# Windowed attention and spectral feed-forward on one core: the deviation's place, five filter taps of the strip before the last image, and the taps of the last strip

## Chip, cores and metric

The kernel runs on one core of a Trainium2 chip. The metric is device time in microseconds from the first to the last instruction of the launch, with the little that lies around them. Three runs of the kernel before gave 3712.17, 3713.88 and 3715.45 us; the median is 3713.88.

## The reference, cut to what matters

The input is eight images of 384 channels and 64 x 64 points, float32. Two layers follow each other, each added to its input:

```
x = x + attention(group_norm(x))        # windows of 8x8, half of the channels shifted
x = x + feed_forward(group_norm(x))

def feed_forward(x):
    t = einsum('bchw,oc->bohw', x, w_in)
    t = irfft2(rfft2(t in 8x8 patches) * fft_filter)
    t = conv3x3(t, w_dw, one filter per channel, zero padding)
    x1, x2 = t[:, :192], t[:, 192:]
    return einsum('bchw,oc->bohw', gelu(x1) * x2, w_out)
```

The change touches only the second layer: its group norm (mean and deviation over groups of channels), the 3x3 filter with its nine taps per channel, and where these stand against each other.

## The kernel before

**Tiling.** An image is cut into NS = 8 strips of eight rows (512 points). The 384 channels are KC = 3 chunks m = 0, 1, 2 of 128 partitions. A pair (b, s) below is image b (0 to 7) and strip s (0 to 7).

**Order by hand.** Every piece of work is a function that is put into a plan with `at(place, piece, ...)`, where `place` is a number; the plan is sorted by it (L811) and the pieces are emitted in that order. An image has 16 units. The feed-forward part of image b runs beside the attention part of image b + 1, so for the last image (B - 1 = 7) it runs alone. Matrix instructions keep the program's order on TensorE (`matmul` and `transpose`, L61 to L73). For the other engines a list scheduler of the compiler decides, by its own estimate of when each instruction is ready, in what order an engine gets them; once it has decided, each engine works in order.

**The second group norm.** `second_mean` (L559) aggregates the statistics on VectorE, averages them over a group with a small matmul (`pm`) and makes a variance in a few one-column VectorE steps (`group_mean`, L241). `second_std` (L562, `group_std` L255) sends this through another matmul (`pv_`, L257), a square root on ScalarE (`sd`, L260), a reciprocal and a shift on VectorE (`sh`, L566). In the plan they stand at first + 1.25 and first + 1.90, where `first` is the unit at which an image's attention ends. For image 7 the second place comes before `back(6, 7)`, which stands at first + 1.99.

**One strip of the feed-forward part** has these steps:

- `normal_x1` (L568): three ScalarE activations to `xn`, after the deviation is known.
- `mix` (L577), four groups: matmuls to `pt`, copied to `t1` by ScalarE (L584).
- `transform` (L588), two halves: small matmuls to `pf`; VectorE multiplies by the filter into `t` (L601), four instructions.
- `back` (L605): 96 small matmuls to `pz`, one PSUM tile for each chunk, in the order 0 and 2 together, then 1. `border` (L621) copies each to a padded tile `z` on ScalarE (L629), gives the strip above its lower border row (L632), and takes the row above for the upper border (L633).
- `conv` (L658): tap by tap. The centre tap is a ScalarE activation (L667), the other eight are VectorE instructions that multiply and add (L673). `TAPS` (L638) lists the taps in the order in which they are used, centre first. Taps 6 to 8 read the row below, so they wait for the next strip.
- `gate` (L683): gelu on ScalarE (L686, L687), products on VectorE (L688 to L690).
- `finish` (L693): matmuls to `pw`, and three VectorE additions to the residual (L712, L714), then the store (L715).

**Taps on TensorE.** In the last image, some taps are matmuls with diagonal matrices: `conv_taps` (L649) sums them in PSUM, in the tile `pc`. `on_pe` (L639) says for each strip how many taps of which chunk; `conv` skips these and begins from `pc`. In strips 0 to 6 of image 7 these are five taps of chunk 1; in strip 7 all nine of chunk 1 first, and then three of chunk 2. `conv_taps(b, s)` stands at u + 2.3 (u is the strip's own unit), which is after the first of the next strip's four `mix` groups. `tap_matrices` (L642) makes the diagonal matrices with one ScalarE activation each (L646), in a strip buffer of the tag "y", of which there are three.

**PSUM.** Tiles come from two rings: four of one bank ("gemm": `pt`, `pf`, `pz`, `pw`, `pm`, `pv_`) and two of two banks ("att": `pc`, the third part of `pw`, and in attention the scores and others).

**Instruction counts.** The planner at L811 to L827 counts TensorE's instructions up to certain places (`small_tiles`, L299) and fills in empty ones (L67) so that runs of small matmuls begin at chosen positions. `conv_taps` counts there with four instructions for each tap (L814).

Of the kernel before, what the change touches and what calls it, by code (L numbers as in the profile page):

```python
# [8 lines left out]
AF = mybir.ActivationFunctionType  # L9
# [3 lines left out]
P = 128  # L13
# [5 lines left out]
NS = SW // WS  # L19
# [11 lines left out]
FETCHES = {"qk_tile": 12, "v_tile": 24, "project": 12, "scores": 128, "apply": 128, "turn": 16, "put": 16,  # L31
           "ln_sums": 64, "mix": 12, "transform": 32, "back": 192, "finish": 48, "input_mean": 4,
           "input_std": 4, "second_mean": 4, "second_std": 4, "filter_weights": 4, "out_bias": 36,
           "qk_weights": 48, "v_weights": 60}
# [4 lines left out]
def block_kernel(ctx: ExitStack, tc: tile.TileContext, out, x, consts, fsel, wqk, wv, bqk, bv,  # L39
                 wp, bp, lng, lnb, rpb1, rpb2, w_in, w_dw, w_out, filt):  # L40
    nc = tc.nc
    B = x.shape[0]
# [10 lines left out]
    def psum2(name):  # L53

        return ps.tile([P, 2, ST], F32, tag="att", bufs=2, name=name)
# [19 lines left out]
    def strip(tag, bufs, name):  # L75
        return sb.tile([P, KC, ST], F32, tag=tag, bufs=bufs, name=name)
# [12 lines left out]
    for s in range(NS):  # L89
        tag, bufs = ("x", 5) if s < 5 else (("xn", 1), ("ow", 1), ("y2", 1))[s - 5]  # L90
        t = strip(tag, bufs, f"x_first{s}")
# [4 lines left out]
    ident = cst[:, C_ID:C_ID + P]  # L96
# [48 lines left out]
    dw_sb = cp.tile([P, KC, 9], F32, name="dw_sb")  # L145
# [131 lines left out]
    def at(place, piece, *args):  # L277
        plan.append((place, len(plan), piece, args))

    xs, ys, y2s, qks, vs, os_, ots, x1s, zs = ({} for _ in range(9))  # L280
# [355 lines left out]


    TAPS = (4, 0, 1, 2, 3, 5, 6, 7, 8)  # L638
    on_pe = {s: {1: 5} for s in range(NS)}  # L639
    on_pe[NS - 1] = {1: 9, 2: 3}  # L640

    def tap_matrices():  # L642
        d = strip("y", 3, "taps").rearrange("p k (t c) -> p (k t) c", c=P)
        for m, n, to in ((1, 9, 0), (2, 3, 9)):
            for i in range(n):
                nc.scalar.activation(d[:, to + i], ident, AF.Copy, scale=dw_sb[:, m, TAPS[i]:TAPS[i] + 1])  # L646
        zs["taps"] = {1: d[:, 0:9], 2: d[:, 9:12]}

    def conv_taps(b, s):  # L649
        pc = psum2(f"pc_{b}_{s}")  # L650
        for i, (m, n) in enumerate(on_pe[s].items()):
            zs[b, s, "zz", m] = pc[:, i]
            for j in range(n):
                dy, dx = TAPS[j] // 3, TAPS[j] % 3
                matmul(pc[:, i], zs["taps"][m][:, j], zs[b, s, m][:, dy:dy + 8, dx:dx + SW],
                       start=(j == 0), stop=(j == n - 1))

    def conv(b, s, m, tap):  # L658

        z = zs[b, s, m]  # L660
        n = on_pe[s].get(m, 0) if b == B - 1 else 0
        if tap < max(n, 1):
            return
        if tap == max(n, 1):
            zz = row512("zz", 5, f"zz_{b}_{s}_{m}")
            if n == 0:
                nc.scalar.activation(zz.rearrange("p (r c) -> p r c", c=SW), z[:, 1:9, 1:SW + 1], AF.Copy,  # L667
                                     scale=dw_sb[:, m, 4:5])
                zs[b, s, "zz", m] = zz
            zs[b, s, "acc", m] = zz  # L670
        acc, old = zs[b, s, "acc", m], zs[b, s, "zz", m]
        dy, dx = TAPS[tap] // 3, TAPS[tap] % 3
        i = nc.vector.scalar_tensor_tensor(acc.rearrange("p (r c) -> p r c", c=SW),  # L673
                                           z[:, dy:dy + 8, dx:dx + SW], dw_sb[:, m, TAPS[tap]:TAPS[tap] + 1],
                                           old.rearrange("p (r c) -> p r c", c=SW), ALU.mult, ALU.add)

        if b < B - 1 and m and tap == 1:
            tc.keep_in_program_order(i)
        if b < B - 1 and (tap == 6 or m == 0 and tap == 1):
            behind(i, zs["soft"], mybir.DependencyClass.NoSync, "softmax first")  # L680
        zs[b, s, "zz", m] = acc
# [39 lines left out]
    for b in range(B):  # L721
        first = 2 * NS * b

        for s in range(NS):
            u = first - 14.84 + s if b else -10 + 0.1 * s
            at(u, load, b, s, "stats")
            at(u + (0.5 if b else 0.05), input_stats, b, s)
        if b == 0:
            at(-3.02, pack_qk)
            at(-2.9, qk_weights, 0)  # L730
            at(-0.95, v_weights)
            at(-0.94, qk_weights, 1)
            at(-0.9, position_bias, 0)
            at(-0.5, position_bias, 1)
            at(0.2, out_bias)
            at(0.2, filter_weights)
        at(first - 5.8 if b else -8, input_mean, b)
        at(first - 5.4 if b else -7.9, input_std, b)
        for s in range(NS):
            u = first + 2 * s  # L740

            v = u - 4
            at(v - 0.84, load, b, s, "norm")
            at(v + 0.15, group_normal, b, s)
            at(v + 0.45, ln_square, b, s)
            if b:
                at(v + 0.985, small_tiles, v + 1)
            at(v + 0.99, ln_sums, b, s)
            at(v + 1.35, ln_scale, b, s)

            if s:
                at(v + 1.50, shifted_half, b, s - 1, 1)
            else:
                at(u - 1.15, shifted_half, b, NS - 1, 1)
            at(u - 1.2 if s < NS - 1 else v + 1.55, shifted_half, b, s, 0)
            for br in range(2):
                w = u + br
                for t in range(3):
                    at(w - 1 + (0.14, 0.34, 0.55)[t], qk_tile, b, s, br, t)
                for g in range(2):  # L760
                    at(w - 1 + ((0.78, 0.86), (0.67, 0.88))[br][g], v_tile, b, s, br, g)
                at(w + 0.05, scores, b, s, br)
                at(w + 0.12, weights, b, s, br)
                at(w + 0.30, exponent, b, s, br)
                at(w + 0.64, turn, b, s, br)
                at(w + 1.00, apply, b, s, br)
                at(w + 1.07, normalise, b, s, br)
                at(w + 1.23, put, b, s, br)

            if 0 < s < NS - 1:  # L770
                places = [u + 3 + f for f in (0.27, 0.45, 0.70)]
            else:
                places = [first + 2 * NS + f + (0.0 if s else 0.24) for f in (0.36, 0.44, 0.52)]
            at(int(places[0]) - 0.84, load, b, s, "add")
            for m in range(KC):
                at(places[m], project, b, s, m)
            at(places[2] + 0.1, keep, b, s)
            at(int(places[2]) + 1.15, store, b, s)
        first += 2 * NS
        at(first + 1.25, second_mean, b)  # L780
        at(first + 1.90, second_std, b)
        if b == B - 1:
            at(first + 2, tap_matrices)
        for s in range(NS):
            u = first + 2 + 2 * s
            at(u - 0.84, load, b, s, "mix")
            at(u + 0.02, normal_x1, b, s)
            for i in range(4):
                at(u + (0.28, 0.45, 0.60, 0.78)[i], mix, b, s, i)
            for j in range(2):  # L790
                at(u + (0.995, 1.02)[j], transform, b, s, j)
            if b < B - 1:
                at(u + 1.985, small_tiles, u + 2)
            at(u + 1.99, back, b, s)

            for n, m in enumerate((0, 2, 1)):
                for tap in range(1, 6):
                    at(u + (2.62, 3.15, 3.5)[n] + 0.06 * tap, conv, b, s, m, tap)
                for tap in range(6, 9):
                    at(u + 4.2 + 0.25 * (n * 3 + tap - 6) / 9, conv, b, s, m, tap)  # L800
            if b == B - 1:
                at(u + 2.3, conv_taps, b, s)
            at(u + 5.16, load, b, s, "finish")
            at(u + 4.5, gate, b, s)
            at(u + 6.10, finish, b, s)
# [5 lines left out]
    order = [p[2:] for p in sorted(plan, key=lambda p: p[:2])]  # L811
    count, dense, empty = fetched["count"], [], [0] * len(order)
    for i, (piece, args) in enumerate(order):
        count += 4 * sum(on_pe[args[1]].values()) if piece is conv_taps else FETCHES.get(piece.__name__, 0)  # L814
        if piece in (qk_tile, project):
            dense.append(i)
        elif piece is scores:
            dense = []
        elif piece is small_tiles:
            n = (RUN_AT[args[0] % 2] - count - round(WAITS[0] * args[0] + WAITS[1])) % 256  # L820
            if n < 100:
                count += n
                for j in range(n):
                    empty[dense[j % len(dense)]] += 1
# [111 lines left out]
```

## Time and profile before

| what | value |
|---|---|
| median of three runs | 3713.88 us |
| the profiled execution, device time | 3717.37 us |
| its span, first to last instruction | 3715.4 us |
| mean granted TensorE clock | 0.995 |
| busy PE (matmuls) | 3609.1 us, 97% |
| busy DVE (VectorE) | 2844.0 us, 77% |
| busy ACT (ScalarE) | 2383.0 us, 64% |
| busy POOL (GpSimd) | 435.1 us, 12% |
| VectorE taps L673 in the whole run | 1490, 751 ns mean |
| `pc` matmul records (two for each tap) | 94 |
| tap matrices L646 | 12, median 410 ns |

The profile is of one execution, 3.49 us above the median of the three runs. Names in it are those of the engines (PE is TensorE, PEld its weight loads, DVE VectorE, ACT ScalarE, POOL GpSimd, SP the queue of DMA issues) and of the program's tiles. A timeline line has the start in us, the time in us, engine, line, operation, output and inputs, shapes, and how many instructions were merged; in brackets how long the engine was idle before and what ended that. Merged instructions of one kind overlap a little, so the start-to-start time is shorter than the mean duration.

Image 7's feed-forward part takes the last 220 us or so. Its eight last additions and stores come one a strip until the end at 3715.4.

### The profile page before, as it was taken

What the parts mean: (1) busy time and instruction counts of PE and PEld (TensorE: products, weight loads), DVE (VectorE), ACT (ScalarE), POOL (GpSimd) and SP (SyncE); (2) the same over time, 40 slices, a digit from 0 to 9 for tenths busy, and PEclk for the clock granted to TensorE, in tenths of its full rate; (3) what the DMA queues carried; (4) which work ended last, traced back from release to release, by engine and by line L of the source; (5) the groups of instructions that cost most, each with busy time, mean ns of one, the idle gap of its engine ahead of it and who ended that gap; (6) DMA issues with size and microseconds to landing.
All of it is one profiled execution on the core that took longest, in us unless ns stands there. A gap on an engine that the chain in (4) does not pass through costs nothing.

```text
span 3715.4 us, 92922 instructions
## 1 busy us (share of the span) xinstructions
PE 3609.1 (97%) x38528; PEld 2340.4 (63%) x38528; DVE 2844.0 (77%) x4601; ACT 2383.0 (64%) x3946; POOL 435.1 (12%) x776
## 2 busy tenths in 40 slices
PE   4999999999999999999999999999999999999898
PEld 2666666666666666666666666666666666666554
DVE  4555568777887788787887778877788777777898
ACT  1766676666676576675776667676676766676442
POOL 5111111011111011101111011111011111110000
PEclk9999999999999999999999999999999999999999
DMA  4222222233232233222332332323232322222422
GB/s 122 80 89 75 92 100 102 87 111 109 101 123 84 89 134 109 104 94 104 107 130 84 109 106 101 132 82 105 88 131 102 107 89 84 100 81 81 154 103 77
DMA packets 144507, 377.34 MB, mean 102 GB/s; under 512 B 12308, under 2 KB 12900, under 8 KB 144100
## 3 DMA queue, kind: packets, MB, share of 16 engines
q1 hardware_dynamic: 139952, 370.60, 28.4%
q8 instruction: 319, 5.23, 0.6%
q0 software_dynamic: 2048, 0.15, 0.1%
q10 hardware_dynamic: 2100, 0.63, 0.1%
q14 instruction: 88, 0.72, 0.1%
HBM read 270.54 MB, written 100.79 MB: 100 GB/s over the span
## 4 chain that ended last, share of the span: by engine, by line
PE 86%; DVE 6%; DMA 4%; ACT 2%; issue 1%; POOL 0%; SPq 0%; DVEq 0%; ACTq 0%; POOLq 0%
PE pq L62 24%; PE pr L62 13%; PE pvv L62 12%; PE pt L62 12%; PE pw L62 6%; DVE zz L673 3%; PE pS L62 3%; PE pA L62 3%; PE pT L72 3%; PE po L72 3%; PE pz L62 3%; PE pf L62 2%; PE ln L62 2%; DMA x_norm<-in_x_dram 1%; DMA rpb_raw<-in_rpb_dram 1%
## 5 line engine op out<-in xcount | busy, mean ns | idle before, releaser
L673 DVE SCALAR_TENSOR_TENSOR zz<-z,dw_sb,zz 128x512 f32<-128x512 f32 x1490 | 1081.8, 751 | 23.7 <-ACT z L632 11.2
L62 PE MATMUL pq<-y,wqk_sb 128*128 128x512 f32 x2160 | 990.2, 596 | 0.0
L62 PEld LDWEIGHTS pq<-y,wqk_sb 128*128 128x128 f32 x2160 | 402.7, 190 | 437.1 <-issue 403.9
L62 PE MATMUL pt<-wi_sb,xn 128*128 128x384 f32 x1536 | 534.6, 486 | 0.0
L62 PE MATMUL pr<-oT,wp_sb 128*128 128x512 f32 x1152 | 523.1, 592 | 0.4 <-DVE oT L537 0.4
L62 PE MATMUL pvv<-wv_sb,y 128*128 128x192 f32 x2880 | 495.8, 326 | 0.0
L62 PEld LDWEIGHTS pvv<-wv_sb,y 128*128 128x128 f32 x2880 | 471.7, 190 | 36.2 <-issue 22.0
L394 ACT ACTIVATE qab<-pq,bq_sb,cst 96x512 f32<-96x512 f32 (+1 forms) x256 | 197.8, 772 | 401.9 <-PE pq L62 385.0
L62 PEld LDWEIGHTS pt<-wi_sb,xn 128*128 128x128 f32 x1536 | 286.1, 190 | 200.9 <-issue 44.0
L394 ACT ACTIVATE kcd<-pq,vec 32x512 f32<-32x512 f32 x512 | 348.4, 680 | 9.0
L62 PEld LDWEIGHTS pr<-oT,wp_sb 128*128 128x128 f32 x1152 | 211.1, 190 | 223.8 <-issue 212.3
L376 POOL COPY y<-y 128x384 f32<-128x384 f32 x112 | 100.0, 893 | 1529.4 <-PE pvv L62 1035.9
L335 POOL TENSOR_TENSOR sq<-sq 128x512 f32<-128x512 f32 x128 | 164.3, 1283 | 638.2 <-ACT sq L333 633.3
L584 ACT COPY t<-pt 128x384 f32<-128x384 f32 x256 | 124.1, 485 | 177.7 <-PE pt L62 174.5
L667 ACT ACTIVATE zz<-z,dw_sb 128x512 f32<-128x512 f32 x183 | 134.0, 733 | 159.0 <-PE pw L62 144.5
L349 DVE TENSOR_TENSOR lr<-m 128x128 f32<-128x128 f32 x64 | 19.7, 308 | 278.3 <-ACT m L347 278.3
L394 ACT ACTIVATE qcd<-pq,bq_sb,cst 96x512 f32<-96x512 f32 (+1 forms) x256 | 197.1, 770 | 44.4 <-PE pq L62 40.9
L428 ACT COPY v<-pvv 128x384 f32<-128x384 f32 x256 | 120.7, 477 | 160.2 <-PE pvv L62 159.2
L546 DVE SCALAR_TENSOR_TENSOR x_add<-pr,vec,x_add 128x512 f32<-128x512 f32 x192 | 143.4, 747 | 94.3 <-PE pr L62 92.6
L62 PE MATMUL pw<-zz,wo_sb 128*128 128x512 f32 (+1 forms) x512 | 182.4, 499 | 0.0
L394 ACT ACTIVATE kab<-pq,vec 96x512 f32<-96x512 f32 (+1 forms) x256 | 174.2, 680 | 9.0 <-PE pq L62 7.4
L72 PEld LDWEIGHTS pT<-cst,e 128*128 128x128 f32 x1024 | 119.1, 141 | 67.2 <-issue 39.8
(140 smaller groups left out, 5297.2 us busy)
## 6 DMA issues: line engine op xcount, KB each, us to landing
x_add<-in_x_dram SPq DMA_DIRECT2D x64, 768.0 KB
x1d<-x_add SPq DMA_DIRECT2D x64, 768.0 KB
x_mix<-x1d SPq DMA_DIRECT2D x64, 768.0 KB
x_finish<-x1d SPq DMA_DIRECT2D x64, 768.0 KB
out_dram<-x_finish SPq DMA_DIRECT2D x64, 768.0 KB
x_norm<-in_x_dram SPq DMA_DIRECT2D x61, 768.0 KB
x_stats<-in_x_dram SPq DMA_DIRECT2D x56, 768.0 KB
rs<-line SPq DMA_DIRECT2D x62, 256.0 KB
```

The costliest lines, as they stand in the source:

```text
L62: tc.keep_in_program_order(nc.tensor.matmul(*args, **kw))
L72: tc.keep_in_program_order(nc.tensor.transpose(*args, **kw))
L335: nc.gpsimd.tensor_tensor(sq[:, 0, :], sq[:, 0, :], sq[:, k, :], ALU.add)
L349: nc.vector.tensor_tensor(rc, m[:, 0:P], m[:, 0:P], ALU.mult)
L376: nc.gpsimd.tensor_copy(dst[:, :, :, :, 0:4], src[:, :, :, :, 4:8])
L394: return nc.scalar.activation(dst[to:to + n], pq[of:of + n], AF.Identity, bias=bias[of:of + n], scale=scale)
L428: nc.scalar.copy(v[:, 2 * g:2 * g + 2, :, 0:HD], pvv[:, 0:384].rearrange("p (g h d) -> p g h d", g=2, h=4))
L546: nc.vector.scalar_tensor_tensor(t[:, m, :], pr, bp_sb[:, m:m + 1], t[:, m, :], ALU.add, ALU.add)
L584: nc.scalar.copy(t1, pt[:, 0:C])
L667: nc.scalar.activation(zz.rearrange("p (r c) -> p r c", c=SW), z[:, 1:9, 1:SW + 1], AF.Copy, scale=dw_sb[:, m, 4:5])
L673: i = nc.vector.scalar_tensor_tensor(acc.rearrange("p (r c) -> p r c", c=SW), z[:, dy:dy + 8, dx:dx + SW], dw_sb[:, m, TAPS[tap]:TAPS[tap] ...
```

## The change

Three edits are made together.

- For image 7, `second_std` moves from first + 1.90 to first + 1.995, which is behind `back(6, 7)` (first + 1.99) and the instruction-count place between them, and before `tap_matrices` and `normal_x1(7, 0)`.
- `on_pe` gets pairs (image, strip) as keys. Strip (6, 7), the last of image 6, which was wholly on ScalarE and VectorE, now has five taps of chunk 1 on TensorE as well. `conv_taps(6, 7)` stands between the first and the second `mix` group of (7, 0).
- In the last strip (7, 7) TensorE takes five taps of chunk 2 in place of three, and these come before chunk 1's nine. `tap_matrices` makes 14 matrices in place of 12, in two buffers of the tag "y" in place of one.

```diff
     TAPS = (4, 0, 1, 2, 3, 5, 6, 7, 8)
-    on_pe = {s: {1: 5} for s in range(NS)}
-    on_pe[NS - 1] = {1: 9, 2: 3}
+    on_pe = {(B - 1, s): {1: 5} for s in range(NS - 1)}
+    on_pe[B - 2, NS - 1] = {1: 5}
+    on_pe[B - 1, NS - 1] = {2: 5, 1: 9}
 
     def tap_matrices():
         d = strip("y", 3, "taps").rearrange("p k (t c) -> p (k t) c", c=P)
-        for m, n, to in ((1, 9, 0), (2, 3, 9)):
+        d2 = strip("y", 3, "taps2").rearrange("p k (t c) -> p (k t) c", c=P)
+        for m, n, to in ((1, 9, d), (2, 5, d2)):
             for i in range(n):
-                nc.scalar.activation(d[:, to + i], ident, AF.Copy, scale=dw_sb[:, m, TAPS[i]:TAPS[i] + 1])
-        zs["taps"] = {1: d[:, 0:9], 2: d[:, 9:12]}
+                nc.scalar.activation(to[:, i], ident, AF.Copy, scale=dw_sb[:, m, TAPS[i]:TAPS[i] + 1])
+        zs["taps"] = {1: d[:, 0:9], 2: d2}
 
     def conv_taps(b, s):
         pc = psum2(f"pc_{b}_{s}")
-        for i, (m, n) in enumerate(on_pe[s].items()):
+        for i, (m, n) in enumerate(on_pe[b, s].items()):
...
     def conv(b, s, m, tap):
 
         z = zs[b, s, m]
-        n = on_pe[s].get(m, 0) if b == B - 1 else 0
+        n = on_pe.get((b, s), {}).get(m, 0)
...
         at(first + 1.25, second_mean, b)
-        at(first + 1.90, second_std, b)
+        at(first + (1.90 if b < B - 1 else 1.995), second_std, b)
...
-            if b == B - 1:
+            if (b, s) in on_pe:
                 at(u + 2.3, conv_taps, b, s)
...
-        count += 4 * sum(on_pe[args[1]].values()) if piece is conv_taps else FETCHES.get(piece.__name__, 0)
+        count += 4 * sum(on_pe[args].values()) if piece is conv_taps else FETCHES.get(piece.__name__, 0)
```

## The prediction

> **What bounds the kernel now.** The page gives TensorE 97% of the span, but the change acts only on the last 220 us, so I read first the busy time by stretch (columns: stretch, its length, then busy us and instruction count of PE, PEld, DVE, ACT, POOL, then granted clock, DMA share, GB/s).
>
> ```profile
> 3350.00:3400.00 50.00, 50.00 (x553) 32.82 (x552) 37.34 (x58) 32.38 (x56) 3.75 (x8) 1.00 0.23 80
> ...
> 3500.00:3550.00 50.00, 40.04 (x391) 25.82 (x393) 49.26 (x81) 21.50 (x41) 0.15 (x1) 0.90 0.45 161
> 3550.00:3600.00 50.00, 48.18 (x483) 29.39 (x476) 44.51 (x71) 22.71 (x53) 0.00 (x0) 0.97 0.30 109
> ```
>
> Up to 3450 TensorE is full. In 3500 to 3550, the seam before image 7's feed-forward part, VectorE is full and TensorE lacks 10 us, and its clock drops. Then I read the timeline of TensorE at the seam.
>
> ```profile
> 3499.70 0.38 PE L62 MATMUL pm_b<-mv_b,cst 128*128 128x1 f32 x2
> 3504.28 0.56 PE L62 MATMUL pv_b<-gt_b,cst 128*128 128x1 f32 x2 [4.19 <-DVE gt_b L252]
> 3504.77 3.68 PE L62 MATMUL pz<-cst,t 64*64 64x64 f32 x96
> ...
> 3520.79 1.53 PE L62 MATMUL pf<-t,cst 64*64 64x192 f32 x32
> 3525.55 3.99 PE L62 MATMUL pz<-cst,t 64*64 64x64 f32 x94 [3.23 <-DVE t L601]
> ```
>
> The deviation's matmul pv_b holds the finished work of back(6,7) behind a VectorE chain (4.19 us). The next hole, 3.23 us, is a wait for t(7,0), which VectorE takes only after eight taps:
>
> ```profile
> 3518.70 6.33 DVE L673 SCALAR_TENSOR_TENSOR zz<-z,dw_sb,zz 128x512 f32<-128x512 f32 x8
> 3524.95 1.94 DVE L601 TENSOR_TENSOR t<-pf,feff 128x384 f32<-128x384 f32 x4
> ```
>
> So the seam is bound by VectorE. Last, all engines in the last two strips: a regular strip's hand-over, then the end.
>
> ```profile
> 3657.55 4.72 DVE L673 SCALAR_TENSOR_TENSOR zz<-z,dw_sb,zz 128x512 f32<-128x512 f32 x7 [1.57 <-ACT z L632]
> ...
> 3667.59 6.71 DVE L673 SCALAR_TENSOR_TENSOR zz<-z,dw_sb,zz 128x512 f32<-128x512 f32 x10
> ...
> 3674.88 1.94 DVE L601 TENSOR_TENSOR t<-pf,feff 128x384 f32<-128x384 f32 x4
> ...
> 3678.39 4.73 DVE L673 SCALAR_TENSOR_TENSOR zz<-z,dw_sb,zz 128x512 f32<-128x512 f32 x7 [1.57 <-ACT z L632]
> ...
> 3682.54 10.47 PE L62 MATMUL pc<-z,taps 128*128 128x512 f32 x24
> ...
> 3688.44 6.32 DVE L673 SCALAR_TENSOR_TENSOR zz<-z,dw_sb,zz 128x512 f32<-128x512 f32 x8
> ...
> 3692.94 1.52 PE L62 MATMUL pw<-g,wo_sb 64*64 64x512 f32 x16
> ...
> 3700.83 0.74 DVE L673 SCALAR_TENSOR_TENSOR zz<-z,dw_sb,zz 128x512 f32<-128x512 f32 x1
> 3701.66 0.63 ACT L687 ACTIVATE g<-zz 64x512 f32<-64x512 f32 x1 [6.24 <-DVE zz L673]
> ...
> 3703.07 3.56 PE L62 MATMUL pw<-g,wo_sb 64*64 64x512 f32 x16 [5.83 <-DVE g L688]
> ...
> 3709.64 0.69 DVE L714 TENSOR_TENSOR x_finish<-pw,x_finish 128x512 f32<-128x512 f32 x1 [0.17 <-PE pw L62]
> ```
>
> A strip takes 20.84 us (3657.55 to 3678.39). Ten taps that alternate between chunks take 0.67 us each; eight of one chunk, each on the last one's sum, 0.79. A tap on TensorE is two records of 0.433 us (24 in 10.4), so 0.87. At the end the chain is chunk 2's taps on VectorE, gelu, gate, and then a pw at less than half speed (3.56 for 1.52).
>
> **The change, part by part.** *Matrices.* Fourteen instead of twelve, 0.41 us each on ScalarE, and a second buffer. The twelve ran at 3312 to 3319, long before use, while TensorE was busy 10.00 of each 10 us. The two more should fill in likewise at no cost; uncovered they cost 0.8. The five of the second buffer can come a strip later, still 150 us early. Four more empty instructions of 13 ns follow from the kernel's own count. No DMA is added or moved, nothing passes SP or POOL.
>
> *Deviation behind back(6,7).* The four t before it end at 3501.04 and free its PSUM. A regular strip runs the rest of pz in 1.45 us, so pz ends near 3502.7. pv_b still waits for gt_b (3504.13) and starts at 3504.28 as before; behind it in TensorE's queue stand finish(6,5) and all of image 7. But pz is out of the way: pw can start at 3504.6 and, taking 4.3, end at 3509. The square root on ScalarE now stands near three z evictions. If they go first (to 3504.3) and a table load of 1.28 follows, sd is at 3505.6; before, 2.3 us from sd to the first xn and 2.3 for three gave 3511.3, so now 3510.2. If sd goes first, the evictions hold pw's PSUM to about 3506.6 and pt starts at 3511. Either way pt, before at 3512.95, gains 2 to 2.8; I take 3510.2.
>
> *Five taps of (6,7).* TensorE adds 5 x 0.87 = 4.3 us, after the first of four mix groups. z is there (evicted by 3507). pf comes at 3510.2 + 1.94 + 4.3 + 5.8 = 3522.2, 1.4 later than before; its first half is done at 3523.0. VectorE loses four taps, 4 x 0.67 = 2.7 us, and ScalarE one 0.72 us activation, which has idle time around it. What is late next is t(7,0). Bounds: it keeps its place at 3524.95, or chunk 1's four taps come before it, as they do in regular strips (ten taps, the one that reads pc, then t). By the nearest row, that strip, I take the second: 12 alternating taps from 3518.70, 12 x 0.67, put t at 3526.7. TensorE then idles from 3523.7 to 3527.2 and its clock falls: from t to pw it took 4.29 us here before (3524.95 to 3529.24). So pw(6,6) is at 3531.0, the next pf half 17.2 later as before (3529.24 to 3546.44), and t(7,1) at 3548.4 with 0.17 of hand-over. VectorE would be ready at 3545.3 (19 taps, three adds, three gate products after t), so TensorE decides. From t to the strip's first tap is 3.51, one strip more 20.84: 3572.8, where the trace has 3574.16. **Seam: 1.4 us.** The five strips after it keep their period and pass this on.
>
> *Last strip.* Chunk 2's five taps come first in pc, chunk 1's nine after. Counted in the old times, pc takes 28 x 0.433 = 12.1 to 3694.7 (1.7 more), pw(7,6) another 4.3 to 3699.0. VectorE has 8 + 4 taps in place of 8 + 6, and chunk 2 starts once five taps are done at 3686.9, so the chunks alternate: 3688.44 + 12 x 0.67 = 3696.5, three gate products of 0.7 to 3698.6. So pw(7,7) follows pw(7,6) without a hole at 3699.0 instead of 3703.07: 4.1. No hole, no clock drop: from pw's start to the last add 4.3 instead of 6.57 (3703.07 to 3709.64): 2.2. The 5.8 us from that add to the end stay. **Tail: 6.3 us.**
>
> *The clock.* In this trace the clock stood at 0.50 after holes of 4.19, 3.23 and 5.83 us, and also after one of 2.39 (3547.2 to 3549.6):
>
> ```profile
> 3548.00:3549.00 1.00, 0.00 (x0) 0.00 (x0) 1.00 (x3) 0.38 (x1) 0.00 (x0) 1.00 0.00 0
> 3549.00:3550.00 1.00, 0.41 (x26) 0.41 (x29) 1.00 (x3) 0.00 (x0) 0.00 (x0) 0.99 0.76 111
> 3550.00:3551.00 1.00, 0.72 (x28) 0.53 (x20) 1.00 (x3) 0.00 (x0) 0.00 (x0) 0.50 0.76 295
> ```
>
> The holes of 0.6 us in regular strips leave it at 1.00. The Trainium skill, "TensorE: Matmul & The Clock Gate", Part 1, says that half clock comes after an idle window of some 3.4 us. By that rule a tail that leaves TensorE idle 1.7 us stays fast; by the rows it lies between 0.6 and 2.39 and may lose the 2.2. The rule speaks against me at the seam, where 3.5 us idle is slow by either. With 2.0 idle instead (t in its old place), the rule would leave 3.45 from t to pw, the row 4.29; I keep both as ends.
>
> **The sum.** 1.4 + 6.3 = 7.7 us of the span of 3715.4, giving 3707.7. The profiled run's device time of 3717.37 has 2.0 outside the span, untouched: 3709.7. It stands 3.5 above the median 3713.88, so the forecast in those terms is 3706.2.
>
> **Rivals.** *t keeps its place* (0.25). Before, it came right after chunk 0's eight taps, which speaks for it; the regular strips speak against. t(7,1) is then at 3546.2 (VectorE 3545.9, TensorE 3545.8 to 3546.6), the seam gives 3.6, total 9.9: 3704.0.
>
> *The gate is late at the end* (0.22). VectorE might take the three residual adds of (7,6), which end near 3700, before the gate, or not read chunk 2 until all of pc is done. The old order, with two taps between and behind those adds, speaks for it; the idle engines speak against. pw(7,7) at 3700.7 saves 4.6 with a fast clock, 2.4 with a slow one: 3707.9 or 3710.1.
>
> *The added TensorE taps eat the seam* (0.09): t(7,0) at 3528 gives nothing at the seam, 3707.6.
>
> *The deviation becomes the wait* (0.04), on the other side. ScalarE works in order; if the root is queued behind the gelu pair of gate(6,6) (before to 3514.5) and reloads its table, sd is at 3515.8, pt at 3520.3, pf's half at 3533.1, t(7,1) at 3555.0, the seam 5.2 slower. With the tail at its low end (1.3, two taps) that is 3.9 slower, 3717.8. It turns against the kernel once sd is later than about 3512. Against it: pv_b's matmul is ready eight microseconds before that pair.
>
> My forecast has 0.40. What a measurement can tell from no change is about 0.2%, 7.4 us, so the forecast is only just beyond it: two thirds of its chance, nearly all of the first rival and little else make faster 0.56; slower by that much needs the last rival and more, 0.03; the rest, 0.41, lies within. The range reaches from 3703.0 (the first rival, a little better) to 3710.6 (the slow-clock tail).
>
> **What would show it.** The hole before pv_b shrinks to some 1.6 us with pz ahead of it; twelve taps with one reading pc stand between gate(6,6) and t(7,0); the strips keep 20.84; pc has 28 records in the last strip; no hole before the last pw and a clock of 1.00 to its end. I am wrong if t(7,0) stands elsewhere, if a hole of over 2 us stays before the last pw, or if ScalarE runs sd after the gelu pair.

## The result, and the profile after

| | before | after |
|---|---|---|
| median, us | 3712.44 (3707.72 to 3715.63, 17 runs) | 3705.64 (3703.85 to 3710.05, 17 runs) |
| ratio after / before, 95% interval | | 0.9984 (0.9977 to 0.999) |
| the profiled execution: device time, span, us | 3717.37, 3715.4 | 3707.98, 3705.9 |

The ratio says 5.9 us less (0.0016 x 3712), from 3.7 to 8.5; the two medians differ by 6.8. The spans of the two profiled executions differ by 9.5 us, which is more than the change did; the profiled execution of before (3717.37) is slower than all of its 17 timed runs. Image 6's last strip shows how far the two executions were apart by then: its first filter product `t` (L601) starts at 3494.25 after and at 3499.09 before. Nearly all of that was there far earlier: the same reciprocal of image 6's attention (the 100th of 128 on L503), ahead of anything in which the two programs differ, starts at 2703.28 and 2707.94. So 4.84 us of the 9.5 are taken here as belonging to the execution, not to the kernel. So I measure from that product onward, in two pieces: the **seam**, from it to the first filter tap behind the last strip's z (the row of seven taps with "<-ACT z L632"), and the **tail**, from there to the end of the span.

| us | seam | tail | both |
|---|---|---|---|
| before | 179.30 | 37.01 | 216.31 |
| after | 176.39 | 35.26 | 211.65 |
| gain | 2.91 | 1.75 | 4.66 |

To set a time of after beside one of before, add 4.84. First the busy time by stretch, in the columns of the table before.

```profile
3500.00:3550.00 50.00, 45.78 (x397) 26.71 (x390) 46.49 (x74) 23.16 (x45) 0.00 (x0) 0.97 0.42 152
3550.00:3600.00 50.00, 48.34 (x396) 28.04 (x395) 46.47 (x74) 19.87 (x44) 0.00 (x0) 1.00 0.34 120
```

At the seam TensorE now works 45.78 of 50 us where it worked 40.04, and VectorE is no longer full. Since after is 4.84 us ahead, each window lies that much further into the work than before's, so these rows show a direction, not an amount. The timeline of TensorE has the amounts.

```profile
3495.33 2.54 PE L62 MATMUL pz<-cst,t 64*64 64x64 f32 x96
3499.35 0.38 PE L62 MATMUL pv_b<-gt_b,cst 128*128 128x1 f32 x2 [1.48 <-DVE gt_b L252]
...
3504.97 2.32 PE L62 MATMUL pt<-wi_sb,xn 128*128 128x384 f32 x6 [1.01 <-ACT xn L574]
3507.12 4.46 PE L62 MATMUL pc<-z,taps 128*128 128x512 f32 x10
...
3517.32 1.53 PE L62 MATMUL pf<-t,cst 64*64 64x192 f32 x32
3521.35 3.66 PE L62 MATMUL pz<-cst,t 64*64 64x64 f32 x95 [2.51 <-DVE t L601]
```

The wait before `pv_b` is 1.48 us where it was 4.19, since the 96 matmuls of `pz` now stand ahead of it; `pv_b` itself is no earlier (3504.19 in before's times, 3504.28 then). `pt` of (7,0) is 3.14 us earlier. The five taps, ten records, use that up, and `pf` is 1.37 later. The hole before `pz` of (7,0) is 2.51 where it was 3.23. VectorE's timeline shows why it is not longer.

```profile
3513.29 0.69 DVE L691 TENSOR_TENSOR g<-g,zz 64x512 f32<-64x512 f32 x1
3513.99 0.75 DVE L675 SCALAR_TENSOR_TENSOR zz<-z,dw_sb,zz 128x512 f32<-128x512 f32 x1
3514.66 0.74 DVE L675 SCALAR_TENSOR_TENSOR zz<-z,dw_sb,pc 128x512 f32<-128x512 f32 x1
3515.32 5.51 DVE L675 SCALAR_TENSOR_TENSOR zz<-z,dw_sb,zz 128x512 f32<-128x512 f32 x8
3520.74 1.95 DVE L601 TENSOR_TENSOR t<-pf,feff 128x384 f32<-128x384 f32 x4
...
3542.03 1.95 DVE L601 TENSOR_TENSOR t<-pf,feff 128x384 f32<-128x384 f32 x4 [1.47 <-PE pf L62]
```

Ten taps, with one that reads `pc`, stand between the gate of (6,6) and `t`(7,0), which starts 0.63 us later than before (3525.58 against 3524.95). `t`(7,1) waits 1.47 us for `pf`, so at that point TensorE decides. Last, TensorE and VectorE at the end of the kernel, put together by time.

```profile
3674.79 12.18 PE L62 MATMUL pc<-z,taps 128*128 128x512 f32 x28
3680.69 6.33 DVE L675 SCALAR_TENSOR_TENSOR zz<-z,dw_sb,zz 128x512 f32<-128x512 f32 x8
3687.01 0.75 DVE L675 SCALAR_TENSOR_TENSOR zz<-z,dw_sb,pc 128x512 f32<-128x512 f32 x1
...
3692.13 1.07 PE L62 MATMUL pw<-g,wo_sb 64*64 64x512 f32 x2 [0.93 <-DVE g L690]
3694.17 1.95 PE L62 MATMUL pw<-g,wo_sb 64*64 64x512 f32 x14 [0.97 <-DVE g L691]
3696.04 4.06 PE L62 MATMUL pw<-zz,wo_sb 128*128 128x512 f32 x8
```

VectorE runs chunk 0's eight taps in a row, at 0.79 us each from start to start, and reads chunk 2 from `pc` for the first time at 3687.01. `pc`'s five taps of chunk 2 were done some 4.3 us after 3674.79; its last record ends at 3686.97. The last `pw` is held twice by the gate, and then runs slowly: the clock granted (the third number from the end) falls just there.

```profile
3694.00:3695.00 1.00, 0.83 (x8) 0.35 (x11) 0.11 (x1) 0.00 (x0) 0.00 (x0) 1.00 0.38 145
3695.00:3696.00 1.00, 1.00 (x9) 0.21 (x3) 0.00 (x0) 0.00 (x0) 0.00 (x0) 0.56 1.03 389
3696.00:3697.00 1.00, 1.00 (x4) 0.50 (x2) 0.00 (x0) 0.00 (x0) 0.00 (x0) 0.50 0.69 252
```

### The profile page after: what moved, and what is told of

It is laid out like the page before. It is cut to its first block, busy times and chain, and to the rows that moved or that the text cites. A ratio compares the mean times of both kernels' runs of the same rounds, so it can differ in the third digit from the quotient of the medians.

```text
span 3705.9 us, 92947 instructions
## 1 busy us (share of the span) xinstructions
PE 3610.6 (97%) x38542; PEld 2337.9 (63%) x38542; DVE 2839.0 (77%) x4595; ACT 2382.8 (64%) x3947; POOL 435.2 (12%) x776
## 4 chain that ended last, share of the span: by engine, by line
PE 86%; DVE 6%; DMA 4%; ACT 2%; issue 1%; POOL 0%; SPq 0%; DVEq 0%; ACTq 0%; POOLq 0%
PE pq L62 25%; PE pr L62 13%; PE pvv L62 12%; PE pt L62 12%; PE pw L62 6%; DVE zz L675 3%; PE pS L62 3%; PE pA L62 3%; PE po L72 3%; PE pT L72 3%; PE pz L62 3%; PE pf L62 2%; PE ln L62 2%; DMA x_norm<-in_x_dram 2%; DMA rpb_raw<-in_rpb_dram 1%
```

## The experiments

Every edit is shown against the kernel after, if nothing else is said. Seam and tail come from one profiled execution each, the ratio to before from timed runs. e5 and e7 have one time each, which tells nothing at this size. A seam is known no better than to about 1 us: the six kernels with the same seam (after, e1, e2, e6, e7, e9) range from 175.62 to 176.78, the two with the old one (before, e5) from 179.30 to 180.00.

| | seam | tail | both: gain on 216.31 | median, us (runs) | ratio, 95% interval |
|---|---|---|---|---|---|
| after | 176.39 | 35.26 | 4.66 | 3705.64 (17) | 0.9984 (0.9977 to 0.999) |
| e2 both seam edits | 176.78 | 36.87 | 2.66 | 3710.93 (12) | 0.999 (0.9981 to 0.9998) |
| e3 deviation alone | 177.68 | 37.62 | 1.01 | 3711.76 (12) | 0.9992 (0.9984 to 1.0001) |
| e4 five taps of (6,7) alone | 179.27 | 38.17 | -1.13 | 3713.29 (12) | 1.0 (0.9991 to 1.0008) |
| e5 last strip alone | 180.00 | 33.61 | 2.70 | 3713.45 (1) | |
| e1 after, own bank for chunk 2 | 175.66 | 30.55 | 10.10 | 3703.87 (6) | 0.9972 (0.9961 to 0.9984) |
| e6 own bank, three taps | 176.62 | 32.25 | 7.44 | 3706.01 (11) | 0.9979 (0.997 to 0.9987) |
| e7 gate before the additions | 176.78 | 33.04 | 6.49 | 3706.56 (1) | |
| e8 own bank, filter first | 176.82 | 30.58 | 8.91 | 3704.01 (12) | 0.9975 (0.9966 to 0.9983) |
| e9 own bank, four taps | 175.62 | 31.10 | 9.59 | 3702.99 (11) | 0.9975 (0.9966 to 0.9984) |
| e10 own bank, seven taps of (6,7) | 176.85 | 30.63 | 8.83 | 3703.68 (8) | 0.9976 (0.9966 to 0.9986) |

The gain read from one trace and the ratio, turned into us, agree within 2.0 us in each timed kernel (e1: 10.10 and 10.4; e2: 2.66 and 3.7; e3: 1.01 and 3.0; e4: -1.13 and 0). Much of what is left is the clock: before, e2, e3 and e4 have the same last strip, yet their tails run from 36.87 (e2) to 38.17 (e4), as the last eight records of `pw`, behind the same hole of 5.8 us, take 2.93 us in e2 and 4.25 in e4.

### The last strip: what holds chunk 2

**e1** gives chunk 2 a PSUM tile of one bank, in place of its half of the two-bank tile `pc`, which chunk 1 then has alone. The matmuls, their order and their number stay.

```diff
-            zs[b, s, "zz", m] = pc[:, i]
+            own = psum(f"pc2_{b}_{s}") if m == 2 else pc[:, 0]
+            zs[b, s, "zz", m] = own
...
-                matmul(pc[:, i], zs["taps"]...
+                matmul(own, zs["taps"]...
```

> The changed kernel, but chunk 2's five taps of the last strip get a PSUM tile of their own of one bank, in place of a half of the two-bank tile that they share with chunk 1's nine. Measured from the first filter product t(6,7) to the end of the span, which was 216.31 us before and 211.65 with the change. Theory A: in the last strip VectorE takes chunk 2's taps only after all of pc, because the shared tile ties them to chunk 1's matmuls; with its own tile the two chunks alternate at 0.67 us a tap, the gate is done before pw(7,6) ends, no hole and no clock drop follow, and the tail gains the 6.3 us of the prediction in place of 1.75: about 207.1 us, faster than the changed kernel by some 4.5 us. Theory B: VectorE's amount of work, or the later pw on TensorE, sets the tail whatever the order: within 0.7 us of 211.65.

The timeline of e1's last strip, both engines put together:

```profile
3673.70 12.18 PE L62 MATMUL pc<-z,taps 128*128 128x512 f32 x28
3679.59 0.75 DVE L676 SCALAR_TENSOR_TENSOR zz<-z,dw_sb,zz 128x512 f32<-128x512 f32 x1
3680.25 0.74 DVE L676 SCALAR_TENSOR_TENSOR zz<-z,dw_sb,pc 128x512 f32<-128x512 f32 x1
3680.91 4.72 DVE L676 SCALAR_TENSOR_TENSOR zz<-z,dw_sb,zz 128x512 f32<-128x512 f32 x7
...
3687.23 0.69 DVE L692 TENSOR_TENSOR g<-g,zz 64x512 f32<-64x512 f32 x1
3687.26 2.85 PE L62 MATMUL pw<-zz,wo_sb 128*128 128x512 f32 x8
3690.03 1.55 PE L62 MATMUL pw<-g,wo_sb 64*64 64x512 f32 x16
3690.18 0.69 DVE L693 TENSOR_TENSOR zz<-zz,pc 128x512 f32<-128x512 f32 x1 [0.70 <-ACT zz L689]
3691.52 2.85 PE L62 MATMUL pw<-zz,wo_sb 128*128 128x512 f32 x8
```

Chunk 2 is read from PSUM at 3680.25, 5.6 us before `pc`'s last record ends (3673.70 + 12.18 = 3685.88; the trace calls both tiles `pc`). The chunks alternate at 0.67 us, the gate's first two products are done while the `pw` before is still running, the third (L693) ends at 3690.87, and the last `pw` follows without a hole in 1.55 + 2.85 us. The tail is 6.46 us shorter than before, and the time from `t`(6,7) to the end is 206.21, where 207.1 was expected. So the tie was the tile: by it, the read of one half waits for matmuls into the other. The waits in VectorE's compiled program say the same. TensorE raises its counter to 20262 with chunk 2's fifth tap, and to 20271 with chunk 1's ninth. These are the two instructions that read `pc`, and the counts that they wait for, first in the kernel after, then in e1:

```
L675 TensorScalarPtr zz_7_7_2<-z1,dw_sb,pc_7_7 [waits PE 20271]
L692 TensorTensor zz_7_7_0<-zz_7_7_0,pc_7_7 [waits Activation 3748]

L676 TensorScalarPtr zz_7_7_2<-z1,dw_sb,pc2_7_7 [waits PE 20262]
L693 TensorTensor zz_7_7_0<-zz_7_7_0,pc_7_7 [waits PE 20271, Activation 3749]
```

In after, the read of chunk 2 waits for chunk 1's ninth tap, though the two halves are different banks; in e1 it waits for its own fifth. The second read of after has no wait for TensorE of its own, as the first has already waited for all of the tile. So the wait is one that is written into the program when it is built. The scheduler's order changed with it, though nothing but the tile had changed: in after it puts chunk 0's eight taps ahead of the read. VectorE therefore never stands idle there, and the tie shows in no wait of the profile: it shows as an order.

**e5** is the change of the last strip alone (the deviation back at first + 1.90, no taps of (6,7)).

```diff
-    on_pe[B - 2, NS - 1] = {1: 5}
...
-        at(first + (1.90 if b < B - 1 else 1.995), second_std, b)
+        at(first + 1.90, second_std, b)
```

> Only the last strip's taps changed (five of chunk 2 first, then nine of chunk 1), deviation and strip (6,7) as before. Two lengths: the seam from t(6,7) to the first tap after the last strip's z (179.3 us before, 176.4 with the change), and the tail from there to the end (37.0 before, 35.3 with the change; two more kernels with the old tail gave 36.9 to 38.2). Theory A, the two parts are separate: seam 179.3, tail 35.3 within 0.7, with chunk 2's taps behind all of pc and two holes of about 1 us before and in the last pw. Rival: the tail's gain needs the shifted seam, so the tail is 36.5 or more.

The tail was 33.61, 1.65 less than after's with the same last strip, and below the range of 34.6 to 36.0 that was expected. The holes are the same, what differs is the clock in the `pw` behind them:

```profile
3699.28 1.07 PE L62 MATMUL pw<-g,wo_sb 64*64 64x512 f32 x2 [0.93 <-DVE g L689]
3701.32 1.51 PE L62 MATMUL pw<-g,wo_sb 64*64 64x512 f32 x14 [0.97 <-DVE g L690]
3702.77 2.85 PE L62 MATMUL pw<-zz,wo_sb 128*128 128x512 f32 x8
```

Here the last two rows take 1.51 and 2.85 us, in after 1.95 and 4.06: 1.65 together, all of the difference. The new last strip is worth 1.75 or 3.4 us against the trace of before, by this alone.

**e6** is e1 with the old number, three taps of chunk 2 (still ahead of chunk 1's nine).

```diff
-    on_pe[B - 1, NS - 1] = {2: 5, 1: 9}
+    on_pe[B - 1, NS - 1] = {2: 3, 1: 9}
```

> The changed kernel with chunk 2's PSUM tile of its own, but only the old three taps of chunk 2 on TensorE in the last strip. With five taps and its own tile the tail was 30.6 us, with five and the shared tile 35.3. Theory A, it is the tie to chunk 1's matmuls that cost the prediction its tail, not the number of taps: VectorE has two taps more, 1.3 us, but TensorE's pc is 1.7 us shorter, so the tail stays within 30.4 to 31.6. Rival, the two taps taken from VectorE are what counts: a tail of 32 to 33.5.

The number is the rival's, 32.25 us, with three holes of 0.53 to 0.74 us before parts of the last `pw`, as here the first of them:

```profile
3692.13 1.07 PE L62 MATMUL pw<-g,wo_sb 64*64 64x512 f32 x2 [0.73 <-DVE g L691]
```

The own bank with the old number of taps (and with chunk 2's taps ahead of chunk 1's, where before has them behind) thus brings 4.76 us of tail, the taps without the own bank 1.75 to 3.4, both together 6.46. All of these are counted from before's tail, in which the clock was slow. So both count, and the own bank counts for more.

**e7** leaves the tile as it is and puts the residual additions of (7,6) behind the gate of (7,7) in the plan, a test of the other half of the rival in the prediction.

```diff
-            at(u + 6.10, finish, b, s)
+            at(u + (6.60 if (b, s) == (B - 1, NS - 2) else 6.10), finish, b, s)
```

> The changed kernel (shared tile), with finish(7,6) planned behind gate(7,7), so that one of the residual additions of strip (7,6) goes behind the last gate product on VectorE in place of before it; TensorE's order is the same. With the change the last pw has holes of 0.93 and 0.97 us and the tail is 35.3. Theory A, the second hole is that addition: it falls to 0.4, and the tail to about 34.6; if less idle time also spares the clock drop, to 33.3. Rival, TensorE's own pace or the output's store sets the end: 35.3 unchanged.

The tail is 33.04.

```profile
3692.41 0.69 DVE L690 TENSOR_TENSOR g<-g,zz 64x512 f32<-64x512 f32 x1 [0.15 <-ACT g L689]
3693.13 0.69 DVE L714 TENSOR_TENSOR x_finish<-pw,x_finish 128x512 f32<-128x512 f32 x1
3693.85 0.69 DVE L691 TENSOR_TENSOR g<-g,zz 64x512 f32<-64x512 f32 x1
```

Against e5, which ran at the same full clock, that is 0.57 us, and VectorE's rows give the same: between the gate's two products now stands one addition, not two, and the second product starts 1.44 us after the first (3692.41 to 3693.85) instead of 2.04 in after. So this one addition costs 0.6 us. Two more still stand ahead of the second product, one before the first and one between; what they cost was not run. In e1 all three stand behind the gate's first two products, with no edit to the plan: chunk 2 is done before `pw`(7,6) is, so there is nothing yet to add. What e1 gains over e7, 2.49 us, holds both the tile and those two.

**e9** asks whether e1 takes one tap too many. It is e1 with one less.

```diff
-    on_pe[B - 1, NS - 1] = {2: 5, 1: 9}
+    on_pe[B - 1, NS - 1] = {2: 4, 1: 9}
```

> As the own-bank kernel, with four taps of chunk 2 on TensorE in the last strip instead of five (13 taps in all, 26 records). With five, TensorE set the end: the gate's last product ended at 3687.92 and the last pw could begin at 3690.03, 2.1 us of slack on VectorE. Theory: one tap fewer gives TensorE 0.87 us back and costs VectorE 0.67, so the slack shrinks to 0.6 and TensorE still sets the end: tail 29.7 us (30.55 with five, 32.25 with three), no hole of over 0.3 us before the last pw. Rival: VectorE already sets the end with four, as it does with three: holes of 0.5 us before the last pw and a tail of 30.9 to 31.5.

The rival is right by its number: 31.10, with a hole of 0.99 us, not in front of the last `pw` but inside it.

```profile
3688.94 1.29 PE L62 MATMUL pw<-g,wo_sb 64*64 64x512 f32 x8
3691.22 0.66 PE L62 MATMUL pw<-g,wo_sb 64*64 64x256 f32 x8 [0.99 <-DVE zz L693]
```

The gate's two products are early enough, as I had worked out; what is late is L693, the one that reads chunk 1 from `pc`, behind chunk 0's gelu. I had measured the slack at the wrong instruction: in e1 L693 ends at 3690.87, not 3687.92. The third part of the last `pw` waits for it, as it takes its PSUM from the same ring of two tiles as `pc`: in e1's compiled program its first matmul waits for the count that L693 sets. e9's timed ratio can't be told from e1's.

### The seam: two edits, alone and together

**e2** is both seam edits with the old last strip, **e3** the deviation alone, **e4** the five taps of (6,7) alone.

```diff
e2
-    on_pe[B - 1, NS - 1] = {2: 5, 1: 9}
+    on_pe[B - 1, NS - 1] = {1: 9, 2: 3}
e3, beyond e2
-    on_pe[B - 2, NS - 1] = {1: 5}
e4, beyond e2
-        at(first + (1.90 if b < B - 1 else 1.995), second_std, b)
+        at(first + 1.90, second_std, b)
```

> The deviation's move and the five taps of (6,7), with the last strip as before (chunk 1's nine taps first, then three of chunk 2). From t(6,7) to the end. Theory A, from the changed kernel's trace: the seam alone gives 2.9 us and the last strip the other 1.75: 213.4 us, with pw of the last strip again behind a hole of 5.8 us and slow. Rival: the last strip only shows what it has because the seam shifted it against the clock's window; then the sum does not split like this and this run is off 213.4 by more than 0.7 us.

> Only the deviation moved behind back(6,7). From t(6,7) to the end, 216.31 before. Theory A, VectorE binds the seam: TensorE reaches pf(7,0) about 3 us sooner, but VectorE has the same work before t(7,1), so the time only lengthens the next hole: 215.5 to 216.3 us. Rival, TensorE's hole of 4.2 us was itself the loss: about 213.3 us.

> Only the five taps of (6,7) on TensorE, deviation and last strip as before. From t(6,7) to the end, 216.31 before. Theory A: without the deviation's move the 4.3 us of added matmuls meet a TensorE that is 3 us later, pf(7,0) comes at about 3525.1 in old times and VectorE takes t(7,0) behind twelve taps near 3528, so little is left: 215.1 to 215.8 us; the two edits of the seam are worth more together than one by one. Rival, they add up: 2.7 us of VectorE work removed shows in full, about 213.6 us.

Gains at the seam: 2.52 for both, 1.62 for the deviation, 0.03 for the taps. Both together bring 0.87 more than the sum, which is within what one execution can be off; the timed ratios (3.7 us for both, 3.0 for the deviation, 0 for the taps) do not part e2 from e3 either. e4 missed both of its ranges: 217.44 from `t`(6,7) to the end, where 215.1 to 215.8 was expected and 213.6 was the rival; 1.16 us of that arise in its tail, where the same last `pw` ran at a slower clock than in before. e3 lies 0.2 below its range (215.30, for 215.5 to 216.3). TensorE's timeline of e3 shows what the deviation alone leaves open:

```profile
3505.92 8.13 PE L62 MATMUL pt<-wi_sb,xn 128*128 128x384 f32 x24 [1.01 <-ACT xn L574]
...
3542.31 4.56 PE L62 MATMUL pz<-cst,t 64*64 64x64 f32 x94 [2.41 <-DVE t L601]
3546.56 1.12 PE L62 MATMUL pw<-g,wo_sb 64*64 64x512 f32 x2
...
3549.36 2.85 PE L62 MATMUL pw<-zz,wo_sb 128*128 128x512 f32 x8
```

Before has at the same place:

```profile
3549.59 0.84 PE L62 MATMUL pz<-cst,t 64*64 64x64 f32 x32 [2.39 <-DVE t L601]
3550.72 2.89 PE L62 MATMUL pz<-cst,t 64*64 64x64 f32 x62 [0.28 <-DVE t L601]
...
3554.89 2.85 PE L62 MATMUL pw<-zz,wo_sb 128*128 128x512 f32 x8
```

In e3, `t`(7,0) comes 3.9 us sooner, counted from `t`(6,7), 22.0 against 25.86. The four taps it overtook are still VectorE's work, and a strip later the hole before `pz` of (7,1) is 2.41 us, no shorter than before's 2.39. It ends 3.4 us sooner than before's (47.11 against 50.50 from `t`(6,7)). But from there to the last eight records of `pw` it takes 7.05 us, and 5.30 before: the clock stood at 0.50 for 6.8 us, and for 3.4 before. So half of what the deviation had won was lost to the clock in this execution. And of e4:

```profile
3500.05 0.35 PE L62 MATMUL pv_b<-gt_b,cst 128*128 128x1 f32 x2 [4.20 <-DVE gt_b L252]
...
3523.95 1.30 PE L62 MATMUL pf<-t,cst 64*64 64x192 f32 x14 [2.05 <-ACT t L584]
```

The first hole is as it was, and the 4.3 us of taps come on top of it: `pf` is late. On top of that, half of it waits 2.05 us for ScalarE's copy, which stands behind the gelu in ScalarE's order. So the taps alone bring nothing that can be seen, since `pf` is late; the later deviation gives TensorE the room for them. That they add to the deviation is not shown. Had the clock of e3 stayed down no longer than before's, its gain would be some 3.4 us (an estimate, 1.62 + 7.05 - 5.30), where both edits gave 2.52 to 3.68.

**e8** asks which engine sets the seam in after. It is e1 with chunk 1's taps of (6,7), and taps 6 to 8 of the other chunks, put behind the filter product `t`(7,0) by a dependency on order alone.

```diff
-            nc.vector.tensor_tensor(t2[:, p], pf_[p]...
+            zs["filtered"] = nc.vector.tensor_tensor(t2[:, p], pf_[p]...
...
+        if (b, s) == (B - 2, NS - 1) and tap >= (5 if m == 1 else 6):
+            behind(i, zs["filtered"], mybir.DependencyClass.NoSync, "filter first")
```

> Own PSUM tile for chunk 2 as in the first of these runs (seam 175.7 us, tail 30.6), and in strip (6,7) chunk 0's taps 6 to 8 and chunk 1's taps are ordered behind t(7,0) on VectorE, so that TensorE's hole of 2.5 us before back(7,0) and its slow clock go. Theory A, VectorE's work binds the seam: t(7,0) comes 2.5 us sooner and TensorE with it, but VectorE idles about 1.4 us for pf and has the same taps left before t(7,1): seam 175.5 to 177. Rival, TensorE's chain from t(7,0) to t(7,1) binds: seam about 173.4. The tail is 30.6 in both.

As expected if VectorE sets it: 176.82, and not the 173.4 of a seam that TensorE sets. `t`(7,0) starts 24.00 us after `t`(6,7) instead of 26.49, the hole before its `pz` is gone, and another of 3.10 us opens a strip later, with no idle time of VectorE ahead of `t`(7,1):

```profile
3519.78 0.69 PE L62 MATMUL pz<-cst,t 64*64 64x64 f32 x32 [0.48 <-DVE t L601]
...
3543.05 3.65 PE L62 MATMUL pz<-cst,t 64*64 64x64 f32 x94 [3.10 <-DVE t L601]
```

**e10** then takes work from VectorE: e1 with seven taps of (6,7).

```diff
-    on_pe[B - 2, NS - 1] = {1: 5}
+    on_pe[B - 2, NS - 1] = {1: 7}
```

> As the own-bank kernel, with seven taps of chunk 1 of strip (6,7) on TensorE instead of five. Theory: VectorE's total work sets the seam, and TensorE only waits there (2.50 us before the pz of (7,0)). Two taps fewer take 1.3 us from VectorE and put 1.7 us of TensorE work into that hole, which shrinks to 1 us or less, so that the clock stays at 1.00: from t(6,7) to the last strip's first tap behind its z 174.3 to 175.0 us (175.66 with five here, 176.39 in the kernel after). Rival: TensorE's chain through pf sets it, and two taps more push t(7,0) back: 176.5 to 177.4. The tail should stay at 30.6 in both.

It missed: 176.85, 1.2 us longer than with five. The rows of TensorE, then of VectorE:

```profile
3521.09 0.88 PE L62 MATMUL pf<-t,cst 64*64 64x192 f32 x14 [1.40 <-ACT t L584]
3522.38 0.69 PE L62 MATMUL pz<-cst,t 64*64 64x64 f32 x32 [0.42 <-DVE t L601]
```

```profile
3541.95 1.95 DVE L601 TENSOR_TENSOR t<-pf,feff 128x384 f32<-128x384 f32 x4 [2.02 <-PE pf L62]
```

The hole before `pz` is filled, as meant, but `pf` of (7,0) is pushed back and waits for ScalarE, as in e4, and at `t`(7,1) VectorE stands idle for 2.02 us. So e8 and e10 lie on either side of the balance: with the filter earlier VectorE decides, with more taps on TensorE the chain through `pf` does. They do not lie equally far off. Counted from `t`(6,7), `t`(7,1) starts at 47.03 in e1, 47.28 in e8 and 48.23 in e10. e10 has its whole 1.2 us by then; e8 has 0.25, and the other 0.9 arise behind the hole of 3.10 us, where `pz` runs at half clock.

## Why the prediction was right, and where it was wrong

The forecast of 3706.2 lies 0.56 us from the median of 3705.64, and its gain of 7.7 us within the interval of 3.7 to 8.5. Yet its two terms are not what the runs show: the seam gave about twice its 1.4 us, the last strip a quarter to a half of its 6.3. The agreement is in good part luck: two errors met, and the median of before, from which the forecast was counted, fell from 3713.88 in three runs to 3712.44 in seventeen.

**Matrices: right.** The fourteen ran from 3308.1 to 3364.1, 390 ns each in the median, long before their use.

**Deviation behind back(6,7): right, step by step.** `pv_b` was not to move, and did not (0.09 us). ScalarE took the three z evictions first, then the square root with its table load, which is the order of the two that I had taken. `pt` was put at 3510.2 and came at 3509.81 in before's times. The rival in which the root is queued behind the gelu pair did not occur.

**Five taps of (6,7): the mechanism right, a term too large.** `pf` was put at 3522.2 and came at 3522.16. I let twelve taps follow the gate of (6,6); there were ten, since of chunk 0's eight one ran ahead of the gate and one behind `t`. So `t`(7,0) came at 3525.58, not 3526.7, the hole was 2.51, not 3.5, and `t`(7,1) came at 3546.87, not 3548.4. The seam's gain was 2.91 (2.52 in e2, with a slower clock; 3.64 in e1, at full clock). The rival "t keeps its place" was near by its number (3.6), but not by its order: `t` came 0.63 later, behind chunk 1's taps.

**Last strip: the step that failed** is "chunk 2 starts once five taps are done at 3686.9, so the chunks alternate". Chunk 2 started when all fourteen were done. Of the gate rival I had written "or not read chunk 2 until all of `pc` is done", and gave it 0.22 together with the residual additions. e1 shows that this clause is what kept the tail from its 6.3 us, and e7 that one of the three additions is worth 0.6 us. The rival had put the tail's gain at 4.6 with a fast clock and 2.4 with a slow one; it measured 3.4 (e5) and 1.75 (after). What I should have asked is not when the data are there but what the program waits for: a tile of two banks is one thing to wait for, and the text of the kernel shows that both chunks share it. With the own bank the same arithmetic came true: 6.46 for 6.3.

**The clock: a range too simple.** I put the limit for a slow clock between holes of 0.6 and 2.39 us. Two holes of 0.93 and 0.97, 1.1 us apart, were enough in after and not in e5; the last section shows that the length of a hole is not all that counts.

**Time.** e1, with the own bank, has the lowest ratio: 0.9972 of before, where the change has 0.9984. Their intervals overlap (0.9961 to 0.9984 and 0.9977 to 0.999), so the timed runs of e1 alone do not show it faster than the change. In the traces it is: the tails of e1, e8 and e10 are alike (30.55, 30.58, 30.63), 3.0 to 4.7 us shorter than those of e5 and after.

## What to carry to other kernels

Before counting on data that are half done, ask what the reader waits for: here two results in one PSUM tile were one wait, and a tile each brought 3.1 to 4.7 us of tail in the traces, about as much as the whole change did. Such a tie can show as an order of instructions on a busy engine and in no wait of the profile, so look at what the engine does first, not only at its idle time. And measure a late change from a fixed point in the trace just ahead of it: here half of the difference between two profiled spans had arisen before the change began. Before laying a small gain to an edit, see whether the clock fell in the one execution and not in the other.

## What the runs showed of the hardware

- **The same hole, with and without a slow clock.** After, e1, e2, e6, e7 and e9 have the same seam, with a hole of 2.50 or 2.51 us before `pz` of (7,0). Behind it `pz` took 3.66 us in after, where the clock was 0.50 for 3.4 us, and 4.00, 3.88 and 3.90 in e2, e6 and e7; in e1 and e9 the clock stayed at 1.00 and it took 2.89. At the end, 1.65 us hung on it. The traces show what decides. Within each of the twelve executions, the clock changes only at instants that lie a whole number of 3.413 us apart. Cut by this grid, the interval that ends in the hole differs from one execution to the next:

| | interval, us | matmuls busy in it, us of 3.41 | clock in the next |
|---|---|---|---|
| e2 | 3520.37 to 3523.78 | 0.76 | 0.50 |
| e7 | 3519.26 to 3522.67 | 0.76 | 0.50 |
| e6 | 3519.81 to 3523.22 | 0.90 | 0.50 |
| after | 3517.62 to 3521.03 | 1.23 | 0.50 |
| e9 | 3516.89 to 3520.30 | 1.39 | 1.00 |
| e1 | 3516.95 to 3520.36 | 1.54 | 1.00 |

Of all such intervals at full clock from 3440 us to the last matmul, the clock fell after each of the 18 with 1.36 us of matmuls or less, and after 2 of the 859 with more: one with 1.65 in e5, and the one that holds the two holes at the end of after, with 2.01 (2.11 in e5, where it did not fall). So what counts is how much of a hole lands in one interval, and a fall then lasts one interval, 3.4 us, or two. Where the grid lies differs between executions: in the table, the intervals start anywhere from 3516.89 to 3520.37 about the same hole. That part of the time is luck. The Trainium skill, "TensorE: Matmul & The Clock Gate", Part 1, has the clock halve after an idle window of some 3.4 us, and says that this window runs freely, so that one kernel warms up after 6, 11 or 14 matmuls from run to run. A free-running window of this length is what these traces show, for the fall too; that it has to be idle throughout they do not show, as with 1.36 us of matmuls in it the clock still fell.
- **A difference that precedes the change.** 4.66 us lie between two executions at 2707 us, where the programs are still the same. Among the twelve profiled executions the product `t`(6,7) starts between 3493.68 and 3499.09. Between before and after the shift builds up along the run: the first reciprocals on L503 are 1.7 us apart, the 43rd 3.7, the 100th 4.7.
